# The order of modulation stores and loads, small loads in front of large ones, the routing's modulation on another engine, and a later ratio, in a fused transformer layer

## The chip, the cores and the metric

The kernel runs on one core of a Trainium2 chip. A core has a matrix engine (TensorE, PE in the profile), a vector engine (VectorE, DVE), an engine for activation functions (ScalarE, ACT), a general one (GpSimd, POOL) and one that issues transfers (SyncE, SP). Each works through its own instructions in order and waits on semaphores for the others. Transfers (DMA) run beside them; here SP and POOL issue nearly all. The metric is the device time of one execution in microseconds, lower is better.

## The reference, cut to what matters

Two layers on x of shape (4, 512, 288) float32 and a condition of shape (4, 288); 16 heads of 18 numbers, 4 experts, the best 2 per token.

```python
mod = silu(c) @ w_adaln + b_adaln
sh_msa, sc_msa, g_msa, sh_mlp, sc_mlp, g_mlp = split(mod, 6)
h = ln(x) * (1 + sc_msa) + sh_msa
q, k, v = h @ w_qkv + b_qkv
o = softmax(q k^T * 18**-0.5) v
x = x + g_msa * (o @ w_proj + b_proj)
xf = ln(x) * (1 + sc_mlp) + sh_mlp
logits = xf @ w_gate ; the two largest per token, softmax over them
moe = sum over the chosen experts of gate * (gelu(xf @ w1 + b1) @ w2 + b2)
x = x + g_mlp * moe
# second layer
U = qr(P).Q ; A = skew matrix filled with silu(cond) @ W.T + b ; R = expm(A)
x = x + (x U R - x U) U^T
```

## The kernel before, in words

The four sequences are called batches; each has four tiles of 128 tokens. x stays in SBUF as `xs`.

*Attention* is a loop over n = 4 b + g (batch b, group g of four heads), and in it over the four tiles t. A step (g, t) issues, in this order: `weigh` (PE's z products at L1779, ACT's exponentials es at L1788), `gather` of the step before (PE's av, L1797), the pieces of work that were put on the list `steps[g, t]`, one piece of the list `beside`, and one scatter (`scatter_next`), two where g is 0 or 3. This order of issue is each engine's order of execution. When the four tiles of a group are done, `normalize` takes the sums of the softmax out through SP (den), DVE takes reciprocals, SP stores them (rdr) and loads them spread over partitions (oT, L1833), and DVE multiplies (oT, L1839). When a batch has its four groups, `merge` (L1855 to L1865) multiplies with w_proj (po), DVE applies the gate (og) and POOL adds it to `xs`.

The work of batch b's steps contains the next batch's first layer norm and q, k, v (`beginning`), and the routing of the batch before (`routing`): `norm` at (2,1) with statistics on DVE (mv), four small instructions on POOL (rs, ms, L1169 to L1175), the normalized rows on ACT (xh, L1184) and the modulation on POOL (L1877 and L1880: times modrow, plus modrow, into xr); the logits in two halves at (2,2) and (2,3), each logit one product with a row of w_gate and its sum on DVE (L1921); the choice of experts at (3,0) (g, L1950, is the difference of the two best logits); `ratio` at (3,1), an exponential of it on ACT (L1954); the gates at (3,2). The second batch of a half (batches 0 and 1, batches 2 and 3) also computes `where`, the places of its tokens in a DRAM table `slots`, and then 16 scatters (L2110, indirect DMA on POOL) write the half's tokens there. Batch 2's routing thus runs in batch 3's steps, and batch 3's in the experts' phase.

The shifts, scales and gates of the modulation are computed twice: for the first norm ahead of the loop, and for the rest (`other_modulation`) as pieces of `beside` in batch 0: PE's pr and DVE's modrows (L1269), then `spread`, which takes four rows to DRAM (mdr, L1275) and back to all 128 partitions (modrow and gates, L1276), on POOL's queue. `skew_matrices`, also in `beside`, computes the skew matrices: `loads` issues the 2.27 MB of W (wr, L1295), a memset and two stores (um, udr), and four loads of the bias (brs, L1306), all on POOL's queue; `product` (pa) multiplies wr on PE. After it, in pieces of `beside` through the attention of batches 0 to 2, comes the matrix exponential (lines 1380 to 1500, tiles pw, XY, ph). A QR of P (`column`, L1558 to L1600) goes in pieces on DVE too.

POOL's DMAs use eight completion semaphores in turn, and an issue waits for the one eight before it, if that has not landed; SP's use eight others.

*Experts.* `hidden(i)` (ph, L2427) and `outputs(i)` (pe, L2487) for i = 0 to 7, four experts for each half of the tokens; tokens come from `slots` (xg, `load_slots`, L2166 to L2171, six DMAs; the first expert's on POOL's queue), are transposed on PE (pt, L2205), and results go back by scatter (chosen, L2503). `load_slots` of the first expert comes after all 16 scatters of the first half, at step (2,3) of batch 3. The list `last_merge` (last divisions, the merge of batch 3), then batch 3's routing, then the rest of the QR, are done one piece at a time in between. A last phase rotates the result and writes it (from about 700 us).

Of the kernel before, what the change touches and what calls it, by code (L numbers as in the profile page):

```python
# [13 lines left out]
ALU = mybir.AluOpType  # L14
# [4 lines left out]
P = 128  # L19
# [794 lines left out]
def fast_path(  # L814
# [142 lines left out]
    with ExitStack() as s1:  # L957
# [92 lines left out]
        def late_loads():  # L1050
            badr = ada.tile([P, C], F32, tag="raw", name="badr")
            nc.gpsimd.memset(badr, 0.0)
            badrs.append(badr)
            for i in range(4):
                nc.sync.dma_start(
                    out=badr[i * HQ : i * HQ + B, :],
                    in_=b_adaln[ds((2 + i) * C, C)].partition_broadcast(B),
                )
            for b in range(1, B):
                nc.sync.dma_start(  # L1060
                    out=xs[:, b * NT : (b + 1) * NT, :],
                    in_=x[b].rearrange("(t p) c -> p t c", p=P),
                )
            nc.sync.dma_start(out=bp, in_=b_proj.partition_broadcast(P))
            nc.sync.dma_start(out=wgT, in_=w_gate)
            nc.sync.dma_start(out=b1s, in_=b1T)
            nc.sync.dma_start(out=wp, in_=w_proj.rearrange("g p c -> p g c"))

        def shift_scale(between):
# [181 lines left out]
        def other_modulation():  # L1251

            rows = ada.tile([P, C], F32, name="modrows")
            mdr = dram.tile([4, B, C], F32, name="mdr")
            to = (gates[:, 0], modrow[:, 0], modrow[:, 1], gates[:, 1])

            def product():

                pr = bank([P, N], "pr")
                for k in range(NK):  # L1260
                    for i in range(4):
                        nc.tensor.matmul(
                            pr[ts(i, HQ), :C],
                            scp[:, k, :],
                            wadb[:, k, ts(i, C)],
                            start=(k == 0),
                            stop=(k == NK - 1),
                        )
                nc.vector.tensor_add(rows, pr[:, :C], badrs[0])  # L1269
                one = rows[2 * HQ : 3 * HQ, :]  # L1270
                nc.vector.tensor_scalar_add(one, one, 1.0)

            def spread():
                for i in range(4):
                    nc.gpsimd.dma_start(out=mdr[i], in_=rows[i * HQ : i * HQ + B, :])  # L1275
                    nc.gpsimd.dma_start(out=to[i], in_=mdr[i].partition_broadcast(P))  # L1276

            return [product, spread]

        def skew_matrices(between):  # L1280

            width = NV // 4
            right.close()
            skew = right.enter_context(tc.tile_pool(name="skew", bufs=1, side="right"))
            um = skew.tile([2 * D, BH, D], F32, name="um")
            udr = dram.tile([D, B, D], F32, name="udr")
            wr = skew.tile([CC, NK, NV], F32, name="wr")
            brs = skew.tile([P, width], F32, name="brs")  # L1290
            row = brs

            def loads():
                for i in range(4):
                    nc.gpsimd.dma_start(  # L1295
                        out=wr[:, :, ts(i, width)],
                        in_=wrT[:, ts(i, width)].rearrange("(k p) f -> p k f", p=CC),
                    )
                nc.gpsimd.memset(um, 0.0)
                for h in range(2):  # L1300
                    nc.gpsimd.dma_start(
                        out=udr[:, ts(h, BH), :], in_=um[ts(h, D), :, :]
                    )
                nc.gpsimd.memset(brs, 0.0)
                for i in range(4):
                    nc.gpsimd.dma_start(  # L1306
                        out=brs[i * HQ : i * HQ + B, :],
                        in_=br[ts(i, width)].partition_broadcast(B),
                    )

            def product():
                pa = bank([P, N], "pa")
                for k in range(NK):
                    for i in range(4):
                        nc.tensor.matmul(
                            pa[ts(i, HQ), :width],
                            scp[:, k, :],
                            wr[:, k, ts(i, width)],
                            start=(k == 0),
                            stop=(k == NK - 1),  # L1320
                        )
                nc.vector.tensor_add(row, pa[:, :width], brs)

            def stores(i, half):
                at, count = 0, 0
                for r in range(D - 1):
                    n = D - 1 - r
                    lo, hi = max(at, i * width), min(at + n, (i + 1) * width)
                    count += lo < hi
                    if lo < hi and count % 2 == half:  # L1330
                        nc.sync.dma_start(
                            out=udr[r, :, ds(r + 1 + lo - at, hi - lo)],
                            in_=row[i * HQ : i * HQ + B, ds(lo - i * width, hi - lo)],
                        )
                    at += n

            def load():
                for h in range(2):
                    nc.sync.dma_start(out=um[ts(h, D), :, :], in_=udr[:, ts(h, BH), :])

            def last():
                pt = bank([P, N], "ptA")
                for b in range(BH):
                    for h in range(2):
                        at = ts(h, D)
                        nc.tensor.matmul(
                            pt[at, ts(b, D)],
                            um[at, b, :],
                            ident[at, at],
                            start=True,  # L1350
                            stop=True,
                        )
                nc.vector.tensor_sub(
                    A.rearrange("p b d -> p (b d)"),
                    um.rearrange("p b d -> p (b d)"),
                    pt[:, : BH * D],
                )
                right.close()

            idle = [lambda: None]  # L1360
            return (
                [loads]
                + between
                + [product]
                + [lambda i=i: stores(i // 2, i % 2) for i in range(8)]
                + [load]
                + idle * 2
                + [last]
            )
# [499 lines left out]
        def route(b):  # L1869

            xr = rt.tile([P, NT, ROW], F32, tag="xr", name=f"xr{b}", bufs=B // HALVES)
            parts = statistics(b, 1)

            def norm():
                xh = normalized(b, 1, *parts)
                for t in range(NT):
                    nc.gpsimd.tensor_tensor(  # L1877
                        xh[:, t, :], xh[:, t, :], modrow[:, 1, b, :], ALU.mult
                    )
                    nc.gpsimd.tensor_tensor(  # L1880
                        xr[:, t, :C], xh[:, t, :], modrow[:, 0, b, :], ALU.add
                    )

            return [norm] + choose(b, xr)

        TH = BH * NT
        halves = {}
# [350 lines left out]
        vectors = gate_vectors()  # L2238
        beside = [lambda: None] + other_modulation() + [skew, prefetch]
        chain, basis = triangular()  # L2240
        held, divides = [], {}

        def gather_oldest():
            n, t, es = held.pop(0)
# [15 lines left out]
        def routing(b):  # L2260
            def start():
                norm, logits0, logits1, top, choices, ratio, gates_, *end = route(b)
                also((2, 1), norm)
                also((2, 2), logits0)
                also((2, 3), logits1)
                also((3, 0), top, choices)
                also((3, 1), ratio)
                also((3, 2), gates_, *end[:1])
                also((3, 3), *end[1:])

            return start
# [14 lines left out]
        for n in range(NN):  # L2286
# [47 lines left out]
                also((3, 2), *takes[:3])  # L2334
                also((3, 3), *takes[3:])
            for t in range(NT):
                if (n, t) == (NN - 2, NT - 1):

                    xg0 = load_slots(0, a2, "hT", 1, nc.gpsimd)
                held.append((n, t, weigh(n, t)))  # L2340
                if len(held) > 1:
                    gather_oldest()
                for piece in steps[g, t]:
                    piece()
                if beside:
                    beside.pop(0)()
                scatter_next()
                if g in (0, 3):
                    scatter_next()
        while held:  # L2350
            gather_oldest()
        for piece in beside:
# [5 lines left out]
            lambda: divide(NN - 1),  # L2358
            None,
            *merge(B - 1),  # L2360
        ]

        third.clear()
# [435 lines left out]
```

## Time and profile before

| | us |
|---|---|
| three runs | 729.96, 725.80, 729.78 (median 729.78) |
| profiled execution, its own time | 727.14 |
| span of its trace | 725.4 |
| busy: PE, DVE, ACT, POOL | 675.8, 487.0, 290.4, 251.4 |
| mean granted clock of PE | 0.969 |

The span is cut into stretches below: busy time of each engine, and the clock granted to PE (1.00 is full speed).

```profile
core 0: us, PE busy (x) PEld busy (x) DVE busy (x) ACT busy (x) POOL busy (x), PEclk, DMA share, GB/s
60.00:67.00 7.00, 1.74 (x16) 0.16 (x8) 1.50 (x7) 0.05 (x1) 3.44 (x7) 0.93 1.00 241
67.00:76.00 9.00, 3.85 (x16) 1.30 (x20) 4.10 (x21) 5.66 (x8) 4.91 (x10) 0.50 0.47 106
76.00:84.00 8.00, 8.00 (x68) 2.70 (x64) 6.19 (x30) 3.82 (x6) 7.01 (x14) 0.98 0.95 309
180.00:200.00 20.00, 17.68 (x94) 5.31 (x94) 17.88 (x92) 11.07 (x14) 4.48 (x9) 0.98 0.17 44
200.00:210.00 10.00, 10.00 (x48) 4.82 (x46) 7.67 (x33) 1.94 (x2) 0.89 (x2) 0.70 0.01 2
313.00:324.00 11.00, 1.57 (x6) 1.01 (x6) 9.93 (x49) 2.45 (x6) 7.19 (x9) 0.60 0.36 92
352.00:380.00 28.00, 28.00 (x125) 20.63 (x124) 14.93 (x63) 9.62 (x23) 10.47 (x14) 1.00 0.38 114
```

A row has the stretch, its length, busy time and number of instructions by engine, the granted clock, the share of time that the DMA engines moved data, and their rate. PE is nearly idle around 60 to 76 and 313 to 324 and full in the experts' phase (last row); the clock falls behind such gaps.

### The profile page before, as it was taken

The page shows a single profiled execution, that of the slowest core. Times are in us where ns is not written, and L with a number is a line of the kernel's source. Part 1 is how long each engine was busy: PE and PEld are TensorE (multiplying, and loading weights), DVE is VectorE, ACT ScalarE, POOL GpSimd, SP SyncE. Part 2 cuts the span into 40 slices and gives each one's busy share as a digit, 9 for nine tenths or more (in the row PEclk, how much of TensorE's full clock was granted, in tenths as well). Part 3 has the DMA queues.
Part 4 walks back from the last instruction along what each step waited for, and adds up shares of the span by engine and source line. Part 5 has one row for each costly group of instructions (what it writes and reads, how often), then busy time and mean ns, then how long its engine had stood idle before and what let it go on. Part 6 is the DMA issues. An engine that isn't in the chain of part 4 may idle for free. (4 is left out here: it accounts for less than half of the span.)

```text
span 725.4 us, 11487 instructions
## 1 busy us (share of the span) xinstructions
PE 675.8 (93%) x3563; PEld 391.0 (54%) x3563; DVE 487.0 (67%) x2172; ACT 290.4 (40%) x465; POOL 251.4 (35%) x382
## 2 busy tenths in 40 slices
PE   6994999989898999949999999999999999999985
PEld 5421332434242434215677776777667676667753
DVE  5473658586876995793179888988888885005144
ACT  3464556475528454734233323323232232222231
POOL 3025862461236337760155263522203132121110
PEclk9998899999989999969999999999999999999997
DMA  9457841001100113346152453355344053206053
GB/s 211 143 175 191 256 140 47 27 18 45 48 13 24 31 60 98 92 123 154 36 158 68 138 149 104 95 150 172 75 123 111 12 172 78 90 22 218 17 164 114
DMA packets 70530, 75.48 MB, mean 104 GB/s; under 512 B 33452, under 2 KB 57746, under 8 KB 70458
## 3 DMA queue, kind: packets, MB, share of 16 engines
q1 hardware_dynamic: 60166, 47.78, 24.1%
q0 software_dynamic: 9792, 26.45, 11.9%
q8 instruction: 30, 0.49, 0.3%
q10 hardware_dynamic: 500, 0.42, 0.3%
q14 instruction: 42, 0.34, 0.2%
HBM read 52.13 MB, written 18.23 MB: 97 GB/s over the span
## 5 line engine op out<-in xcount | busy, mean ns | idle before, releaser
L2487 PE MATMUL pe<-w2s,hm 128*128 128x288 f32 (+1 forms) x648 | 163.7, 408 | 0.0
L1788 ACT ACTIVATE es<-z 128x1024 f32<-128x1024 f32 x128 | 124.0, 1020 | 71.9 <-PE z L1779 71.7
L2427 PE MATMUL ph<-xgT,w1s 128*128 128x288 f32 (+2 forms) x576 | 151.8, 413 | 0.4
L2487 PEld LDWEIGHTS pe<-w2s,hm 128*128 128x128 f32 (+1 forms) x648 | 118.7, 187 | 31.5 <-issue 2.3
L2427 PEld LDWEIGHTS ph<-xgT,w1s 128*128 128x128 f32 x576 | 105.8, 190 | 40.0 <-issue 10.8
L1779 PE MATMUL z<-qk 32*128 32x512 f32 x512 | 92.9, 663 | 15.8 <-ACT es L1788 15.8
L2449 ACT ACTIVATE hm<-ph,b1r 128x576 f32<-128x576 f32 (+2 forms) x72 | 49.8, 737 | 130.4 <-PE ph L2440 125.0
L1797 PE MATMUL av<-es,vt 128*32 128x512 f32 x512 | 71.4, 631 | 0.0
L2502 POOL TENSOR_TENSOR y<-y,gb 128x288 f32<-128x288 f32 x32 | 26.1, 817 | 121.5 <-ACT y L2501 121.4
L1779 PEld LDWEIGHTS z<-qk 32*128 32x128 f32 x512 | 27.9, 189 | 60.0 <-ACT es L1788 44.9
L2501 ACT ACTIVATE y<-pe,weight 128x288 f32<-128x288 f32 x32 | 16.0, 501 | 104.0 <-PE pe L2487 104.0
L1741 PE MATMUL pq<-hT,wqk 96*126 96x512 f32 (+3 forms) x120 | 57.3, 615 | 0.0
L2503 POOL DMA_INDIRECT chosen<-y,place x36 | 36.6, 1016 | 53.9 <-DVE y L2499 34.3
L2110 POOL DMA_INDIRECT slots<-xr,where x32 | 32.5, 1016 | 60.4 <-DMA slots<-xr,where 35.6
L1921 DVE SCALAR_TENSOR_TENSOR pl<-xr,wg 128x288 f32<-128x288 f32 x64 | 46.0, 781 | 9.2 <-POOL xr L1880 9.2
L1561 DVE SCALAR_TENSOR_TENSOR q<-q 64x1 f32<-64x1 f32 (+1 forms) x192 | 46.2, 241 | 7.0
L1572 DVE STREAM_SHUFFLE wj<-pt 32x288 f32<-32x288 f32 (+47 forms) x96 | 42.1, 438 | 0.7
L1741 PEld LDWEIGHTS pq<-hT,wqk 96*126 96x126 f32 (+3 forms) x120 | 20.8, 184 | 34.2 <-issue 30.4
L1797 PEld LDWEIGHTS av<-es,vt 128*32 128x32 f32 x512 | 10.3, 110 | 50.4 <-issue 42.6
L1753 POOL DMA_DIRECT2D qk<-row x42 | 21.4, 516 | 45.1 <-ACT row L1748 45.0
L1855 PE MATMUL po<-wp,oT 128*128 128x288 f32 x128 | 34.7, 422 | 1.1 <-DVE oT L1839 1.1
L1839 DVE TENSOR_TENSOR oT<-oraw,oT 128x512 f32<-128x512 f32 x16 | 11.0, 689 | 36.5 <-DMA oT<-rdr 30.4
(281 smaller groups left out, 898.7 us busy)
## 6 DMA issues: line engine op xcount, KB each, us to landing
w2s<-in_w_dram SPq DMA_DIRECT2D x8, 1296.0 KB
w1s<-in_w_dram SPq DMA_DIRECT2D x8, 1152.0 KB
slots<-empty POOLq DMA_DIRECT2D x36, 148.0 KB, 3.5
oT<-rdr SPq DMA_DIRECT2D x64, 64.0 KB
qk<-row POOLq DMA_DIRECT2D x42, 72.0 KB, 2.6
yc<-chosen SPq DMA_DIRECT2D x4, 576.0 KB
out_dram<-xs SPq DMA_DIRECT2D x8, 288.0 KB
wr<-in_wrT_dram POOLq DMA_DIRECT2D x4, 567.0 KB, 8.9
```

Source lines behind the costliest of these rows:

```text
L1561: nc.vector.scalar_tensor_tensor(s, u, part, s, ALU.mult, ALU.add)
L1572: nc.vector.stream_shuffle(wj[o : o + HQ, j:], pt[o0 : o0 + HQ, j:], [j % HQ] * HQ)
L1741: nc.tensor.matmul(pq[:n], wqk[:rows, k, item, :n], hT[:rows, k, :], start=(k == 0), stop=(k == NK - 1),)
L1779: nc.tensor.matmul(zs[c // 2][:, c % 2, :], qk[ts(c, HQ), 1, ts(t, P)], qk[ts(c, HQ), 0, :], start=True, stop=True,)
L1788: nc.scalar.activation(e, z, AF.Exp, scale=SCALE)
L1797: nc.tensor.matmul(avs[n][ts(c, HQ), :], vts[b % 2][:, t, 4 * g + c, :], es[c // 2][:, c % 2, :], start=(t == 0), stop=(t == NT - 1),)
L1855: nc.tensor.matmul(po, oTs[b][:, g, ts(t, P)], wp[:, g, :], start=(g == 0), stop=(g == NG - 1),)
L1921: nc.vector.scalar_tensor_tensor(pr, xr[:, t, :C], 1.0, wg[:, e, :], ALU.mult, ALU.mult, accum_out=lg[:, t, e : e + 1],)
L2427: nc.tensor.matmul(ph[:, j, :SB], w1s[:, k, ts(f, P)], xgT[:, k, ts(j, SB)], start=(k == 0), stop=False,)
L2449: nc.scalar.activation(hm[:, f, : CAPS[r]].rearrange("p (j s) -> p j s", j=NB), ph[:, :, :SB], AF.Gelu_apprx_tanh, bias=b1r[:, h, r, f : f ...
L2487: nc.tensor.matmul(po[ts(m, rows), :], slots_[:, f, :], w[:, f, :], start=(f == 0), stop=(f == NF - 1),)
L2503: nc.gpsimd.indirect_dma_start(out=chosen[h], out_offset=bass.IndirectOffsetOnAxis(ap=place[:, t : t + 1], axis=0), in_=y, in_offset=None, ...
```

## The change

1. In `late_loads` (SP), w_gate, b_proj and b1 come in front of the loads of x for batches 1 to 3.
2. In `spread`, all four stores come first, then the four loads that read them back.
3. In `loads` of the skew matrices, the memset, the two small stores and the four bias loads come first, the four large loads of wr last.
4. In `route`, the modulation (two instructions for each of four tiles) is done by DVE, two tiles at a time in front of each half of the logits.
5. For batch 2 the ratio goes from (3,1) to (3,3), and the gates (`gates_`) to the end of `last_merge`; what follows in that list of pieces comes one piece later.
6. The first expert's `load_slots` goes from step (2,3) to (2,0) of batch 3, and two scatters are issued per step where g is 1, as well as 0 and 3, so that all 16 are issued before it.

```diff
@@ late_loads
+            nc.sync.dma_start(out=wgT, in_=w_gate)
+            nc.sync.dma_start(out=bp, in_=b_proj.partition_broadcast(P))
+            nc.sync.dma_start(out=b1s, in_=b1T)
             for b in range(1, B):
...
-            nc.sync.dma_start(out=bp, in_=b_proj.partition_broadcast(P))
-            nc.sync.dma_start(out=wgT, in_=w_gate)
-            nc.sync.dma_start(out=b1s, in_=b1T)
@@ spread
                 for i in range(4):
                     nc.gpsimd.dma_start(out=mdr[i], in_=rows[i * HQ : i * HQ + B, :])
+                for i in range(4):
                     nc.gpsimd.dma_start(out=to[i], in_=mdr[i].partition_broadcast(P))
@@ skew_matrices, loads
-                for i in range(4):
-                    nc.gpsimd.dma_start(
-                        out=wr[:, :, ts(i, width)],
-                        in_=wrT[:, ts(i, width)].rearrange("(k p) f -> p k f", p=CC),
-                    )
                 nc.gpsimd.memset(um, 0.0)
...
                         in_=br[ts(i, width)].partition_broadcast(B),
+                    )
+                for i in range(4):
+                    nc.gpsimd.dma_start(
+                        out=wr[:, :, ts(i, width)],
+                        in_=wrT[:, ts(i, width)].rearrange("(k p) f -> p k f", p=CC),
                     )
@@ route
             def norm():
-                xh = normalized(b, 1, *parts)
-                for t in range(NT):
-                    nc.gpsimd.tensor_tensor(
-                        xh[:, t, :], xh[:, t, :], modrow[:, 1, b, :], ALU.mult
-                    )
-                    nc.gpsimd.tensor_tensor(
-                        xr[:, t, :C], xh[:, t, :], modrow[:, 0, b, :], ALU.add
-                    )
-
-            return [norm] + choose(b, xr)
+                xhs_.append(normalized(b, 1, *parts))
+
+            def modulated(t):
+                xh = xhs_[0]
+                nc.vector.tensor_mul(xh[:, t, :], xh[:, t, :], modrow[:, 1, b, :])
+                nc.vector.tensor_add(xr[:, t, :C], xh[:, t, :], modrow[:, 0, b, :])
+
+            def with_logits(i, logits):
+                for t in range(i * NT // 2, (i + 1) * NT // 2):
+                    modulated(t)
+                logits()
+
+            chosen_ = choose(b, xr)
+            for i in range(2):
+                chosen_[i] = lambda i=i, logits=chosen_[i]: with_logits(i, logits)
+            return [norm] + chosen_
@@ routing
+                if b == B - 2:
+
+                    also((3, 0), top, choices)
+                    also((3, 3), ratio)
+                    late.append(gates_)
+                    return
@@ attention loop
-                if (n, t) == (NN - 2, NT - 1):
+                if (n, t) == (NN - 2, 0):
 
                     xg0 = load_slots(0, a2, "hT", 1, nc.gpsimd)
...
-                if g in (0, 3):
+                if g in (0, 1, 3):
                     scatter_next()
@@ last_merge
             *merge(B - 1),
+            *late,
         ]
```

More of the change, by code (lines that the diff above doesn't have):

```diff
@@ L1872, in route @@
             parts = statistics(b, 1)
+            xhs_ = []
             def norm():
-                xh = normalized(b, 1, *parts)
-                for t in range(NT):
-                    nc.gpsimd.tensor_tensor(
-                        xh[:, t, :], xh[:, t, :], modrow[:, 1, b, :], ALU.mult
-                    )
-                    nc.gpsimd.tensor_tensor(
-                        xr[:, t, :C], xh[:, t, :], modrow[:, 0, b, :], ALU.add
-                    )
-            return [norm] + choose(b, xr)
+                xhs_.append(normalized(b, 1, *parts))
[11 more added lines that the diff above has]
+            return [norm] + chosen_
         TH = BH * NT
@@ L2240, in fast_path @@
         chain, basis = triangular()
-        held, divides = [], {}
+        held, divides, late = [], {}, []
         def gather_oldest():
```

## Prediction, made before the changed kernel had run

> **What bounds the kernel now.** I read the busy times first, then the waits of TensorE, then each stretch of the timeline where TensorE is idle or its granted clock falls.
>
> ```profile
> PE 675.8 (93%) x3563; PEld 391.0 (54%) x3563; DVE 487.0 (67%) x2172; ACT 290.4 (40%) x465; POOL 251.4 (35%) x382
> PEclk9998899999989999969999999999999999999997
> ```
>
> TensorE (PE) has work for 93% of the span, so the change can pay only in the 50 us without PE work, or where the clock row falls below 9. The waits say which these are.
>
> ```profile
> PE z L1779 <- ACT es L1788: 15.8, 13, 10.4
> PE pt L2205 <- DVE q L1558: 7.0, 1, 7.0
> PE pt L2205 <- DMA xg<-slots: 2.7, 1, 2.7
> PE ph L1436 <- DVE XY L1474: 2.1, 1, 2.1
> PE pt L1205 <- DVE pw L1452: 1.3, 1, 1.3
> PE pt L1205 <- DVE XY L1488: 0.9, 1, 0.9
> ```
>
> So one wait of 10.4 us on ACT, three small ones on DVE (4.3 us together), and 9.7 us in front of the experts (L2205). The timeline by engine at the first and the last place:
>
> ```profile
> 56.47 2.75 POOL L1295 DMA_DIRECT2D wr<-in_wrT_dram  x4 [0.35 <-PE av L1797]
> 63.91 0.52 POOL L1306 DMA_DIRECT2D brs<-in_br_dram  x1 [1.21 <-DMA wr<-in_wrT_dram]
> 69.00 2.18 ACT L1184 ACTIVATE xh<-xs,ms,rs 128x288 f32<-128x288 f32 x4 [8.96 <-POOL ms L1175]
> 72.14 2.98 PE L1779 MATMUL z<-qk 32*128 32x512 f32 x8 [10.41 <-ACT es L1788]
> ...
> 297.70 0.24 POOL L1175 TENSOR_SCALAR ms<-ms 128x4 f32<-128x4 f32 x1
> 316.54 0.21 ACT L1954 ACTIVATE g<-g 128x4 f32<-128x4 f32 x1 [5.99 <-DVE g L1950]
> 314.73 0.93 POOL L2166 DMA_DIRECT2D xg<-slots  x1 [3.98 <-DMA slots<-xr,where]
> ```
>
> (Start, duration, engine, instruction; in brackets the idle time before it and who ended it.) At 60 us POOL is held by the small brs loads, which wait for wr's landings, so its four statistics instructions (rs, ms) are late, ACT's xh is late, and with ACT in order the softmax behind it. From 60 to 72 PE does 1.7 us of work, and the granted clock is 0.50 from 66.5 to 76.2. At 313 ACT waits 5.99 us for the routing's g; the experts' first tokens (xg) wait behind the scatters.
>
> **Start of attention.** The interleaved store-load pairs (39.2 to 55.6) go in a row: four stores at 0.6 us to 41.6, then four loads at 0.6 us. The first store landed 2.0 us after its issue ended, so the loads run 42.1 to 44.6 instead of ending at 56.1. um, udr and two brs loads follow to about 48; two more brs and the wr loads each reuse a completion flag of a load eight earlier, which landed 4.2 and 3.9 us after issue before. wr's first issue is thus 49.3 and its last ends by 53.5 (in before 56.47 to 63.9). rs starts there, ms comes 2 us later: 55.5, and with wr issued as late as 57 still 59.7. ACT is free for xh at 60.05, so its wait goes. z follows xh by 3.14 us in before (69.00 to 72.14): z at 63.2, 9.0 us earlier, and the 1.3 us that half clock cost up to 79 go too: **-10.2**.
>
> What is late next: wr itself. Its 2.27 MB took 14 us from first issue to quiet engines (56.5 to 70.5). From 49.3 that is 63.3, from 53.5 it is 67.5; the skew product that reads it came 4.4 us behind z's restart, now 67 or so. Nearer to the early end, as the first two issues alone keep the engines busy: nothing lost, at worst 4 us. Moving small loads in front of x's loads at 30 us: three issues of 0.4 to 0.7 us, 1.6 us; batch 1's statistics ended at 53.3 and are not used before 53.5: nothing.
>
> [...]
>
> **Routing of batches 0 and 1.** Eight modulation instructions per batch go from POOL to DVE, each pair in front of its logits.
>
> ```profile
> 150.03 1.03 DVE L1921 SCALAR_TENSOR_TENSOR pl<-xr,wg 128x288 f32<-128x288 f32 x1 [2.05 <-POOL xr L1880]
> 161.09 0.45 DVE L1921 SCALAR_TENSOR_TENSOR pl<-xr,wg 128x288 f32<-128x288 f32 x1
> 158.14 0.64 PE L1205 MATMUL pt<-ident,xh 128*96 128x128 f32 x4 [1.27 <-DVE pw L1452]
> 199.75 0.69 PE L1436 MATMUL ph<-XY,pw 64*64 64x64 f32 x8 [2.15 <-DVE XY L1474]
> ```
>
> The same logit takes 1.03 us while POOL runs its TENSOR_TENSORs and 0.45 (0.385 from start to start) once POOL has stopped. So 16 x 0.385 = 6.2 plus 8 x 0.40 = 3.2 (from DVE's 0.69 us for 512 columns; 0.46 for 288 in L1864) is 9.4 us, against 15.0 (148.0 to 163.0) now: DVE is 5 us ahead from there. The waits of 1.27 and 2.15 us go: DVE runs without a gap from 179 to 205, starting behind the oT of 179.15, whose chain moves by 4.4 us. With the second goes the clock of 0.50 that the windows show from 199.6 to 206; at half clock the eight av matmuls took 1.94 instead of 1.06, so about 2.5 of the 6.4 us. For batch 1 the wait of 0.94 us at 236 goes: **-1.3 -2.15 -2.5 -0.9 = -6.9**. Bounds: if the two waits are set by other chains, only -2; not below -9.
>
> [...] The idle 2.15 us was enough for the 6.4 us at 0.50. [...]
>
> **End of attention.** Three things move. The ratio of batch 2 goes two steps later and its gates behind the last merge: ACT's 5.99 us wait goes, three small DVE pieces (1.4 us) enter phase 2, under PE work. Modulation leaves POOL (7.3 us). And the first expert's loads, six issues, 7.3 us, go from step (2,3) to (2,0) of the last group pair, behind all 16 scatters of the first half; for that two scatters go per step in g = 1 as well. In POOL's order the last three scatters and two residual additions now stand in front of the rs and ms of batch 2.
>
> ```profile
> 294.87 1.01 POOL L2110 DMA_INDIRECT slots<-xr,where  x1 [1.17 <-DMA slots<-xr,where]
> 298.90 2.17 ACT L1184 ACTIVATE xh<-xs,ms,rs 128x288 f32<-128x288 f32 x4
> 347.11 0.69 DVE L1839 TENSOR_TENSOR oT<-oraw,oT 128x512 f32<-128x512 f32 x1 [5.17 <-DMA oT<-rdr]
> ```
>
> Each scatter waits for the one before: 1.0 issued and 1.8 landing, 2.8 us. Three more make 8.4, less 2 us of holes already there: ms at 304.3 instead of 297.94, and xh, without wait at 298.90 now, waits **5.4 us**, PE's softmax step behind it; some 6 us of PE idle. In return, of the 10.4 us in front of the experts all but a little goes: the experts start near 324.7 instead of 330.55, 5.9 earlier. But the merge of batch 3, 16 us into them, needs the last oT (347.11), which hangs on a chain of divisions and small DMAs (recip at 325.4, stores, loads, recip at 336, stores, loads) behind the last attention steps. PE reaches that product (346.47) just in time now, so it would come 3 to 5 us too early, and only 0.6 to 2.6 us of the 5.9 stay, with a half-clock stretch to pay (up to 2.5 us, as above). I take **0** (-3 to +3).
>
> From there to the end PE is full (20 of 20 us per window), POOL and DVE have slack there, and the last 25 us are the same chain: everything before shifts through.
>
> **Sum.** -10.2 - 6.9 + 0 = -17.1 on the profiled execution's 727.14 us (span 725.4): 710.0. That execution lies 2.6 us under the median of the runs shown (729.78) and 1.3 over the lowest; I put the forecast at 711.
>
> **Rivals.**
> *End of attention repaired too.* If scatters shrink behind the earlier `where`, and ms is not later, the 10.4 us and their half clock (0.50 to 328.6) go: -12.9 more, 698. Against it: the 2.8 us cadence in every pair of scatters; for it: where moves 0.7 to 1.7 us ahead of PE.
> *wr's landing becomes the wait.* If the loads to modrow and gates land late, now four together, wr's flags come late; at 57 as the first issue wr is there at 71, and the skew product costs 4 us and a half clock of 1 to 3. Then -4 to -6 from the first stage: 715 to 717; with routing's lower bound, 720.
> *DVE becomes the bound* (slower). If the 1.03 us is not POOL's doing but these operands', modulation costs as much: 24 x 0.97 = 23 us per routing instead of 15. Then PE waits 8 us more at 158, at 236 and at the end, with 2.5 of half clock each, +31 against -10: 748. It decides from 19 us per routing (0.79 per instruction), where three times 4 us more eat the first stage. Against it: 0.45 as soon as POOL stops.
> *The change does nothing where it counts*: POOL stays held by another flag, statistics as late as now: 725 to 732.
>
> **From these to the numbers.** Chances: forecast 0.52; full repair 0.15; wr late 0.20; DVE bound 0.06; nothing 0.07. The forecast's own range is 705 to 716. Downwards the range takes half of the repair (700), upwards all of wr late with routing's lower bound and some spread between runs (723); out remain half of the repair, DVE and nothing: 0.2. One per cent, 7.3 us, is about what a measurement of this kernel tells from no change. Faster by more: 0.52 + 0.15 + most of wr late (0.15), 0.82; within: 0.11; slower: 0.07.
>
> **What would show it.** Right: no wait of ACT's xh near 60, z of step (2,2) near 63, clock near 1 from 60 to 80; logits at 0.4 us in every routing, no wait at XY; a new wait of about 5 us of ACT on ms near 285, the 7.0 and 2.7 us waits gone, and one of 3 to 5 us at po in front of the last oT. Wrong: skew's product waiting for wr, logits still at 1 us, or scatters closer than 2.8 us.

## The result, and the profile after

The changed kernel took 724.03 us (median of 20 runs, 720.63 to 728.21), the kernel before 727.75 us (20 runs, 722.37 to 729.96): a ratio of 0.9957, with a 95% interval of 0.9939 to 0.9976. That is 3 us faster, real but small; 711 us (700 to 723) were predicted. The profiled execution of the changed kernel has a span of 723.0 us, against 725.4.

The waits of TensorE in the changed kernel (what waited, for whom; us in total, times, longest):

```profile
PE z L1780 <- ACT es L1789: 14.1, 14, 8.2
PE po L1856 <- DVE oT L1840: 9.2, 3, 6.6
PE pt L1205 <- DVE brs L1323: 5.6, 1, 5.6
```

All the waits that the change was predicted to remove are gone: the 10.4 us on es, the 2.1, 1.3 and 0.9 us on VectorE, the 9.7 us in front of the experts. Three others stand in their place: 8.2 us on es at another spot, 6.6 us on the last oT, and 5.6 us on the addition of the skew product (brs). The first was foreseen at 6 us, the second at 3 to 5 us, the third not at all.

Where the gain went can be followed by the start of the same TensorE instruction in the two traces:

| TensorE instruction | before | after | difference |
|---|---|---|---|
| first z (no part of the change has acted yet) | 28.05 | 26.72 | -1.3 |
| z, first after the long wait | 72.14 | 61.75 | -10.4 |
| skew product pa | 76.55 | 65.42 | -11.1 |
| z two steps on | 82.27 | 72.12 | -10.2 |
| z after the transposes | 89.99 | 86.74 | -3.2 |
| z in batch 1 | 163.28 | 159.86 | -3.4 |
| z in batch 2 | 209.19 | 202.29 | -6.9 |
| z in batch 3, ahead of the norm of batch 2 | 298.18 | 290.17 | -8.0 |
| the next z, behind it | 302.03 | 301.41 | -0.6 |
| first product of the experts | 330.55 | 318.89 | -11.7 |
| po, second tile of the last merge | 350.66 | 347.81 | -2.9 |
| end of the span | 725.4 | 723.0 | -2.4 |

The 1.3 us at the top are there before anything differs between the kernels and belong to the execution, so each later difference has that much less of the change in it. Nine us were won at 62 us, seven of them lost by 87; five were won in the routings; seven lost at 300; eleven won back in front of the experts, nine of them lost at po. Less the 1.3 us, these two traces end 1.1 us apart, the medians 3.7: a single pair of executions is no better than that.

The first loss, in the timelines of GpSimd, SyncE, VectorE and TensorE of the changed kernel (start, duration, engine, instruction, idle time before it and who ended it):

```profile
50.99 0.73 POOL L1307 DMA_DIRECT2D wr<-in_wrT_dram  x1 [0.96 <-DMA modrow<-mdr]
53.86 2.02 POOL L1307 DMA_DIRECT2D wr<-in_wrT_dram  x3 [2.14 <-DMA gates<-mdr]
57.77 0.25 POOL L1175 TENSOR_SCALAR ms<-ms 128x4 f32<-128x4 f32 x1
...
56.07 0.35 SPq L1826 DMA_DIRECT2D rdr<-den  x1
65.84 1.72 SPq L1834 DMA_DIRECT2D oT<-rdr  x4
...
72.38 0.69 DVE L1840 TENSOR_TENSOR oT<-oraw,oT 128x512 f32<-128x512 f32 x1 [10.34 <-DMA oT<-rdr]
79.39 0.68 DVE L1323 TENSOR_TENSOR brs<-pa,brs 128x504 f32<-128x504 f32 x1 [0.18 <-DMA slots<-empty]
...
61.75 2.04 PE L1780 MATMUL z<-qk 32*128 32x512 f32 x8 [1.35 <-ACT es L1789]
65.42 3.69 PE L1316 MATMUL pa<-wr,scp 96*32 96x504 f32 x24
80.13 1.09 PE L1205 MATMUL pt<-ident,xh 128*96 128x128 f32 x4 [5.65 <-DVE brs L1323]
```

W is issued at 51 to 56 us, ms is ready at 58, z starts at 61.75 and pa does not wait: as predicted. But the 8 KB store rdr of the first division, issued at 56.07, has landed only when the oT loads can be issued at 65.84, and these only at 72.38. VectorE stands 10.34 us in front of that division, and behind it in its order are a QR column, the next group's reciprocal and the addition that empties pa's bank. TensorE's transposes need that bank at 74.5 and get it at 80.1.

The second loss, in the timelines of GpSimd, ScalarE and TensorE, and the third, in those of SyncE, VectorE and TensorE, of the changed kernel:

```profile
294.90 0.98 POOL L2119 DMA_INDIRECT slots<-xr,where  x1 [1.78 <-DMA slots<-xr,where]
297.69 0.54 POOL L1175 TENSOR_SCALAR ms<-ms 128x4 f32<-128x4 f32 x1
298.27 2.18 ACT L1184 ACTIVATE xh<-xs,ms,rs 128x288 f32<-128x288 f32 x4 [7.26 <-POOL ms L1175]
301.41 2.98 PE L1780 MATMUL z<-qk 32*128 32x512 f32 x8 [8.22 <-ACT es L1789]
...
329.51 0.57 SPq L1826 DMA_DIRECT2D rdr<-den  x1
330.17 0.38 SPq L2175 DMA_DIRECT2D xg<-slots  x1
330.60 7.60 SPq L2177 DMA_DIRECT2D xg<-slots  x4
338.88 1.86 SPq L1834 DMA_DIRECT2D oT<-rdr  x4
342.40 0.69 DVE L1840 TENSOR_TENSOR oT<-oraw,oT 128x512 f32<-128x512 f32 x1 [7.26 <-DMA oT<-rdr]
343.15 1.33 PE L1856 MATMUL po<-wp,oT 128*128 128x288 f32 x2 [6.62 <-DVE oT L1840]
```

ms stands behind the sixteenth scatter. And the four loads of the last oT stand on SP's queue behind six loads of the second expert's tokens, which take 8.6 us to issue.

### The profile page after: what moved, and what is told of

The parts are those of the page before. It is cut to its first block, busy times and chain, and to the rows that moved or that the text cites. A ratio compares the mean times of both kernels' runs of the same rounds, so it can differ in the third digit from the quotient of the medians.

```text
span 723.0 us, 11477 instructions
## 1 busy us (share of the span) xinstructions
PE 674.6 (93%) x3563; PEld 391.4 (54%) x3563; DVE 485.3 (67%) x2204; ACT 290.2 (40%) x465; POOL 223.3 (31%) x350
## 5 line engine op out<-in xcount | busy, mean ns | idle before, releaser
L1780 PE MATMUL z<-qk 32*128 32x512 f32 x512 | 90.7, 650 | 14.1 <-ACT es L1789 14.1
L1562 DVE SCALAR_TENSOR_TENSOR q<-q 64x1 f32<-64x1 f32 (+1 forms) x192 | 44.3, 231 | 7.0
L1798 PEld LDWEIGHTS av<-es,vt 128*32 128x32 f32 x512 | 10.2, 109 | 48.8 <-issue 40.3
L1856 PEld LDWEIGHTS po<-wp,oT 128*128 128x128 f32 x128 | 23.5, 191 | 22.4 <-DVE oT L1840 10.6
```

The costliest lines, as they stand in the source:

```text
L1562: nc.vector.scalar_tensor_tensor(s, u, part, s, ALU.mult, ALU.add)
L1780: nc.tensor.matmul(zs[c // 2][:, c % 2, :], qk[ts(c, HQ), 1, ts(t, P)], qk[ts(c, HQ), 0, :], start=True, stop=True,)
L1798: nc.tensor.matmul(avs[n][ts(c, HQ), :], vts[b % 2][:, t, 4 * g + c, :], es[c // 2][:, c % 2, :], start=(t == 0), stop=(t == NT - 1),)
L1856: nc.tensor.matmul(po, oTs[b][:, g, ts(t, P)], wp[:, g, :], start=(g == 0), stop=(g == NG - 1),)
```

## Experiments

Times below are medians; ratios are to runs of the kernel before on the same chip (725.0 to 727.9 us), with 95% intervals. The changed kernel has 0.9957 (0.9939 to 0.9976). Four runs (the divisions behind the addition, a third of W, the last oT first, four together) ran where the kernel before had 725.0 us, 2.7 less than beside the changed kernel; for these the differences to the changed kernel are taken from the ratios.

**Only the transfers' order.** The kernel before with the first three hunks of the change's diff (`late_loads`, `spread`, `loads`), of which the core is

```diff
                 for i in range(4):
                     nc.gpsimd.dma_start(out=mdr[i], in_=rows[i * HQ : i * HQ + B, :])
+                for i in range(4):
                     nc.gpsimd.dma_start(out=to[i], in_=mdr[i].partition_broadcast(P))
```

> The kernel before with only the transfers' order changed (parts 1 to 3). Theory: TensorE's attention steps come 10 us earlier from 62 us on, but only some 3.2 us are left from 90 us on, as in the changed kernel (z at 128.1 for 131.3 before): VectorE stands at its first division until the small loads behind W have landed (72 us), and the addition that frees the skew product's bank comes behind that. Time: 3 us under the kernel before. Rival, as predicted: the 10 us go through to the end, 10 us under it.

723.3 us, 0.9944 (0.9913 to 0.9975), 4 us under the kernel before. The wait at the addition is there:

The waits of TensorE in this kernel:

```profile
PE pt L2206 <- DVE q L1559: 6.8, 1, 6.8
PE pt L1205 <- DVE brs L1323: 6.8, 1, 6.8
```

Of the 10 us only 3 to 4 stay, as the theory had it; going through to the end would have been 717. The 6.8 us in front of the experts are still there too.

**Only the modulation on VectorE.** The kernel before with the hunk of `route`:

```diff
-                    nc.gpsimd.tensor_tensor(
-                        xh[:, t, :], xh[:, t, :], modrow[:, 1, b, :], ALU.mult
-                    )
...
+                nc.vector.tensor_mul(xh[:, t, :], xh[:, t, :], modrow[:, 1, b, :])
```

> The kernel before with only the routing's modulation on VectorE (part 4). Theory: logits at 0.45 us, no wait of TensorE at pw or XY, 4.5 to 5 us won by 240 us; and with GpSimd free of it at 302 to 310, the last scatters end and the first expert's loads issue some 7 us earlier with no new wait of ms, another 3 to 6 us. Time: 8 to 11 us under the kernel before, more than the whole change. Rival, that the end of attention is bound by something else and gives all back: 4 to 5 us under it or the same.

716.3 us, 0.985 (0.979 to 0.991): 11 us under the kernel before and 8 under the changed kernel. This one part is worth more than the whole change. The windows of this kernel behind 200 us (length; busy time by engine; granted clock; DMA share; GB/s):

```profile
200.00:210.00 10.00, 8.21 (x43) 4.60 (x40) 7.99 (x31) 3.27 (x4) 2.21 (x4) 1.00 0.02 2
```

The clock is 1.00 here, 0.70 before: the half clock behind XY's wait is gone. At the end of attention, without part 6, GpSimd's last scatter is issued at 299.9 us (309.7 before) and the first expert's loads at 303.3 (314.7), with no new wait on ms.

**Part 6 taken back.**

```diff
-                if (n, t) == (NN - 2, 0):
+                if (n, t) == (NN - 2, NT - 1):
...
-                if g in (0, 1, 3):
+                if g in (0, 3):
```

> The changed kernel with part 6 taken back (scatters at the old pace, the first expert's loads at step (2,3)). Theory: three scatters fewer stand in front of rs and ms, so ScalarE's wait of 7.3 us and TensorE's of 8.2 us near 293 us go; a wait for xg of up to 5 us comes in front of the experts, and the last division comes 5 to 8 us earlier. Time: 4 to 9 us under the changed kernel. Rival, that the early loads are worth what the scatters cost: the same as the changed kernel or slower.

717.0 us, 0.986 (0.979 to 0.993), 7 us under the changed kernel. GpSimd's and ScalarE's timelines in this kernel:

```profile
291.61 0.24 POOL L1175 TENSOR_SCALAR ms<-ms 128x4 f32<-128x4 f32 x1
292.32 1.10 POOL L2119 DMA_INDIRECT slots<-xr,where  x1 [0.47 <-issue]
...
292.15 2.18 ACT L1184 ACTIVATE xh<-xs,ms,rs 128x288 f32<-128x288 f32 x4
```

ms comes 6 us earlier, ScalarE does not wait, and TensorE waits 7.0 us (4.3 and 2.7) in front of the first expert's tokens instead. The place of the scatters is the cause of the second loss.

**The QR column behind the addition.**

```diff
-                    for step in ((1, 0), (1, 3), (2, 1), (2, 3)):
+                    for step in ((1, 0), (1, 3), (2, 3)):
                         also(step, column)
...
+                if b == 0:
+                    also((3, 3), column)
```

> The changed kernel with one QR column of batch 0 (5.7 us on VectorE), which stands between the late division and the addition of the skew product, moved from step (2,1) to (3,3). Theory: the addition follows the division of 72.4 us within 2 us instead of 7, TensorE's wait of 5.65 us at the transposes and the half clock behind it go, 6 to 7 us earlier from 90 us on. Time: 5 to 7 us under the changed kernel. Rival, that these transposes wait for W or for the clock and not for VectorE's order: the same as the changed kernel.

722.2 us, 0.9921 (0.9895 to 0.9947): 2 us under the changed kernel, where 5 to 7 were expected, and the intervals overlap. The wait fell from 5.65 to 2.71 us, not to nothing: behind the division (72.2) the reciprocal waited until 74.8 for the next group's sums, whose loads are queued on SP behind the late oT loads. So it is VectorE's order that TensorE waits for, and it is not the column alone.

**The divisions behind the addition.**

```diff
+                    if (b, i) == (0, 2):
+                        for m in (0, 1):
+                            also((2, 3), lambda m=m: divide(m))
+                        continue
+                    if (b, i) == (0, 3):
+                        also((3, 0), lambda: divide(1))
+                        also((3, 1), lambda: divide(1))
...
```

> The changed kernel with the first two groups' divisions put behind the addition of the skew product in VectorE's order (steps (2,3) to (3,1) of batch 0). Theory: the addition follows the product (69.1 us), TensorE's wait at the transposes (5.65 us, 2.7 with only the column moved) goes wholly with its half clock, and z of batch 1's first steps comes 6 to 7 us earlier than in the changed kernel; 3 to 6 us under it in the end, since the end of attention keeps part. Rival, that the transposes wait for something else too: as with the column moved, 2 to 3 us.

Two of its four executions took 723.4 and 724.2 us, the other two 949.5 and 2044.0 us, for which nothing in its profile gives a reason; the kernel before had 725.0 us there, and only the profile is used. The addition ran at 69.07, the wait at the transposes was gone and z came at 79.58 instead of 86.74, as expected. But none of it reached the end. TensorE's timeline in batch 1:

```profile
124.30 4.71 PE L1856 MATMUL po<-wp,oT 128*128 128x288 f32 x10 [6.00 <-DVE oT L1840]
```

The first batch's merge waits for its last division. That chain (VectorE's reciprocals, SyncE's small transfers) was hardly made earlier (124.30 for 125.47 in the changed kernel); only TensorE was let past it. The edit itself also puts two divisions later, so this run alone does not show where the chain would end without it. What it does show is that letting one consumer past the queue uncovers the next.

**A third of W.** This leaves out two thirds of W's loads; the product multiplies one third three times, so the rotations differ.

```diff
-                        out=wr[:, :, ts(i, width)],
-                        in_=wrT[:, ts(i, width)].rearrange("(k p) f -> p k f", p=CC),
+                        out=wr[:, 0, ts(i, width)],
+                        in_=wrT[:CC, ts(i, width)],
```

> The changed kernel with a third of W loaded (0.76 MB for 2.27; the skew product multiplies that third three times, so the rotations differ). Theory: the small stores and loads of the divisions (rdr, oT) then land soon after their issue near 56 us, VectorE's first division comes before 66 us instead of at 72.4, the addition of the skew product right behind it, and TensorE's wait of 5.65 us with its half clock is gone: 6 to 7 us earlier from 90 us on; 4 to 7 us under the changed kernel in the end. Rival, that W's bytes do not hold the small ones: the division near 72 us as now, and the same time.

716.6 us, 0.9884 (0.9807 to 0.9962): by the ratios 5 us under the changed kernel, though the two intervals just overlap. SyncE's and VectorE's timelines in this kernel:

```profile
55.34 0.35 SPq L1826 DMA_DIRECT2D rdr<-den  x1
57.58 1.72 SPq L1834 DMA_DIRECT2D oT<-rdr  x4
...
64.07 0.69 DVE L1840 TENSOR_TENSOR oT<-oraw,oT 128x512 f32<-128x512 f32 x1 [2.98 <-DMA oT<-rdr]
71.00 0.68 DVE L1323 TENSOR_TENSOR brs<-pa,brs 128x504 f32<-128x504 f32 x1 [0.19 <-DMA slots<-empty]
```

rdr to oT takes 2.2 us instead of 9.8, VectorE divides at 64.07 instead of 72.38, TensorE does not wait at the transposes, and the gain stays: the first merge product comes 10.0 us earlier than before (3.2 in the changed kernel). With the same order and fewer bytes the loss is gone, so it is W's burst that holds the small transfers.

**W early and alone.** The four broadcast loads of the modulation go behind rs, ms and the gate weights; W follows the four modulation stores and the two stores of udr, ahead of the loads of the bias.

```diff
+            def back():
                 for i in range(4):
                     nc.gpsimd.dma_start(out=to[i], in_=mdr[i].partition_broadcast(P))
...
+                for i in range(4):
+                    nc.gpsimd.dma_start(
+                        out=wr[:, :, ts(i, width)],
...
+        vectors[1] = lambda turn=vectors[1]: (turn(), back())
```

> The changed kernel with the whole W, issued right behind the four modulation stores (near 42 us instead of 51 to 56), and the four broadcast loads of the modulation (2.3 MB) behind rs and ms and the gate weights (near 60 us). Theory: W has landed before the first division's store is issued (56 us), so rdr and oT land in their usual 2 to 5 us, VectorE divides before 66 us, and TensorE's wait of 5.65 us is gone as with a third of W: z of the step at 86.7 comes at 80; 5 to 8 us under the changed kernel, near 717. Rival, that any 2 MB beside the division do the same (now the broadcast loads): the division near 70 us again and the time of the changed kernel.

722.1 us, 0.9931 (0.9893 to 0.9968), 2 us under the changed kernel with overlapping intervals, where 5 to 8 were expected. W went out at 45.4 to 48.1, and rdr to oT took 1.4 us (59.42 to 60.86), as the theory says. But W now covered the loads of the sums (VectorE waited 6.99 us for den, until 59.14), and the broadcast loads at 61 to 63 us covered oT (69.30). The division came near 70 us again, as the rival has it: in this run the small transfers beside either large load were late. Between 45 and 70 us there are 5.1 MB of large ones (four of 567 KB, five of 576). TensorE's wait at the transposes fell to 2.6 us.

**The last oT first on SP's queue.**

```diff
-                if m == 1 and i + 1 < HALVES * E:
+                if i and m == 1 and i + 1 < HALVES * E:
                     xg = load_slots(i + 1, hp, "xg", 1)
                 if rest and (piece := rest.pop(0)):
                     piece()
+                if not i and m == 1:
+                    xg = load_slots(i + 1, hp, "xg", 1)
```

> The changed kernel with the four loads of the last oT issued on SP's queue in front of the second expert's six loads instead of behind them. Theory: the last division comes some 7 us earlier (335 for 342.4), TensorE's wait of 6.6 us at po and the half clock behind it go; 5 to 9 us under the changed kernel. Rival, that the last oT hangs on the division's sums and not on SP's order: the same as the changed kernel.

720.1 us, 0.9928 (0.9892 to 0.9965): by the ratios 2 us under the changed kernel with overlapping intervals, so the time alone shows no gain (one execution of ten took 1302 us, unexplained). The wait at po fell from 6.62 to 3.78 us. It is the queue, as the theory says, but less of it than the 7 us expected. What is left is the store in front of oT: rdr is issued at 331.05, half a us behind the 1.3 MB load of the second matrix (w2s), whose traffic ends near 336.2, and oT can be issued only at 337.52. It looks like the start of attention again, a small transfer beside a large one; the best kernel below moves that load too.

**Four of these together.** The divisions behind the addition, part 6 taken back, the last oT first, and the first expert's weights one step later.

```diff
-                weights = [expert_weights(0)]
+                weights = []
+                also((3, 1), lambda: weights.append(expert_weights(0)))
```

> The changed kernel with the divisions behind the addition, part 6 taken back, the last oT's loads in front of the second expert's, and the first expert's weights issued one step later (they start with the last scatter, whose landing they delay). Theory: the gains of these places add: -6 at the start, -7 from the scatters, -3 from the last oT, 3 or so from the first tokens: 708, 14 to 19 us under the changed kernel. Rival, that each only uncovers the next wait: 715 to 718, as part 6 taken back alone.

716.2 us, 0.9879 (0.9801 to 0.9956), by the ratios 6 us under the changed kernel: the rival. TensorE reached the first expert's tokens at 306.9 and waited 7.48 us for them. The weights moved later did not help: they were now issued at 306.6, among the tokens' own loads (301.4 to 308.6), and the transposes of the tokens could go on at 314.8, with part 6 alone taken back at 313.6.

**W early, and the end of attention rearranged.** Part 6 taken back; the first expert's tokens on SP's queue; the second matrix and the second expert's tokens behind the last oT.

```diff
-                    xg0 = load_slots(0, a2, "hT", 1, nc.gpsimd)
+                    xg0 = load_slots(0, a2, "hT", 1)
...
-        weights2 = [expert_weights2(0)]
+        weights2 = []
...
+                if not i and m == 1:
+                    weights2.append(expert_weights2(0))
+                    xg = load_slots(i + 1, hp, "xg", 1)
```

> The run with W early, and at the end of attention part 6 taken back, the first expert's tokens issued on SP's queue (six issues of 0.4 us there, 0.9 on GpSimd's), and the second matrix and the second expert's tokens behind the last oT. Theory: no wait of ScalarE on ms, TensorE's wait for xg 2 to 4 us instead of 7, none at po; 702 to 708, 16 to 22 us under the changed kernel. Rival, that the waits only change their place: 710 to 717.

710.0 us, 0.9749 (0.971 to 0.9789): 14 us under the changed kernel and 18 under the kernel before, the best of all, but short of the 702 to 708 expected and at the edge of the rival's range. The waits on ms and for xg are gone; those at po are not: 1.6 us are left at the last oT, and 4.3 us at the first batch's merge. SyncE's and TensorE's timelines:

```profile
299.49 0.39 SPq L2177 DMA_DIRECT2D xg<-slots  x1
299.93 3.46 SPq L2179 DMA_DIRECT2D xg<-slots  x4
...
306.92 0.63 PE L2216 MATMUL pt<-ident,xg 128*128 128x128 f32 x4 [0.34 <-DMA xg<-slots]
```

With the last, at 303.43, six issues take 4.5 us on SP's queue instead of 7.3 on GpSimd's, and the tokens cost TensorE 0.34 us.

**Part 5 taken back, twice.** Parts 1 to 4 only (parts 5 and 6 taken back), and the best kernel without part 5:

```diff
-                if b == B - 2:
...
-                    also((3, 3), ratio)
-                    late.append(gates_)
-                    return
```

> The changed kernel with parts 5 and 6 taken back (the kernel before with parts 1 to 4). Theory: parts 5 and 6 are what costs, and of them part 6: 716 to 718, as with part 6 alone taken back (717.0). Rival, that part 5 is worth something by itself: 720 or more; or that parts 1 to 3 and part 4 add (4 and 11 us): 712 to 713.

> The run with W early and the end of attention rearranged (710.0), with part 5 taken back as well, so that of the change parts 1, 2, 3 and 4 are left. Parts 1 to 4 alone had 714.6 and part 6 alone taken back 717.0, their intervals overlapping. Theory: part 5 is worth nothing where ScalarE does not wait for it: 709 to 711. Rival: it costs the 2 to 3 us between those two: 706 to 708.

Parts 1 to 4 took 714.6 us, 0.9818 (0.9769 to 0.9868), 9 us under the changed kernel; so parts 5 and 6 together cost 9 us, and part 6 alone 7 (717.0). Whether part 5 cost the rest cannot be told from those intervals. In the best kernel neither expectation held: without part 5 it took 715.0 us, 0.9826 (0.9784 to 0.9868), 5 us more. ScalarE's and TensorE's timelines without part 5:

```profile
311.20 0.20 ACT L1965 ACTIVATE g<-g 128x4 f32<-128x4 f32 x1 [8.50 <-DVE g L1961]
...
312.37 2.99 PE L1782 MATMUL z<-qk 32*128 32x512 f32 x8 [5.53 <-ACT es L1791]
```

Where the tokens were late, the ratio's wait showed no cost, since TensorE waited in front of them anyway (4.6 and 2.7 us with parts 1 to 4 only); with the tokens there at 306, ScalarE's wait for g at (3,1) is what TensorE waits for, 5.5 us. Part 5 is worth 5 us there, with the other wait gone.

## Why the prediction was wrong, point by point

*Start of attention, predicted -10.2, measured -1.9 (the -3.2 of the table less the 1.3 of the execution).* The mechanism was right to within a microsecond as far as it went: stores at 0.6 us, the waits on modrow's and gates' flags (1.05, 0.96 and 2.14 us), ms at 57.8 (predicted 55.5, at most 59.7), z at 61.75 (63.2), pa at 65.4 with no wait for W. The step that failed is "what is late next: wr itself", answered with "nothing lost, at worst 4 us". It asked only when W lands for its own product. That small loads amid W took 10 us could be seen in the trace before (oT's four loads of 64 KB were issued from 59.98 to 61.90, and VectorE could divide at 71.50); the question who waits for them, and who is queued behind that waiter on VectorE, was not asked. VectorE's timeline in the kernel before had the answer:

```profile
71.50 0.69 DVE L1839 TENSOR_TENSOR oT<-oraw,oT 128x512 f32<-128x512 f32 x1 [9.83 <-DMA oT<-rdr]
79.39 0.68 DVE L1322 TENSOR_TENSOR brs<-pa,brs 128x504 f32<-128x504 f32 x1 [1.15 <-DMA slots<-empty]
```

VectorE stood at the same division until 71.50 (72.38 in the changed kernel), behind the same W, and came to the addition at 78.2. There it waited 1.15 us more; the view names a DMA, but the skew product had ended just then, at 79.26. The change brought the product eleven us forward and left VectorE where it was: the addition starts at 79.39 in both traces. So TensorE could gain only as far as the transposes that need the addition's bank (84.57 before, 80.13 after, -4.4, of which 1.3 are the execution's), and another 1.2 went with the half clock behind the new wait (0.50 from 80 to 84). Moving W did not put it beside the division; it was there already, and the change left it there. The run with a third of W shows it: there the division comes 8 us earlier and 6.8 us come back at the first merge.

In the changed kernel rdr was issued at 56.07, behind all of W (51 to 55.9), W's traffic ends at 64.5 us, and oT is issued at 65.84. In the kernel before the same store went out at 55.86, ahead of W's first load (56.47), and oT could be issued at 59.98; late there were oT's own loads, issued amid W. Whether rdr's own bytes were late or only the signal that they had landed, no run here separates.

*Routings, predicted -6.9, measured -4.8 (from -3.2 to -8.0).* Right in mechanism: the logit takes 0.45 us and the modulation 0.45, all waits of TensorE on pw and XY are gone and the clock is 1.00 where it was 0.70. Sizes: of the 1.3 us, a wait of 0.63 us for hT took half; behind the 2.15 us there came 1.39 us at po. Some of the size is chance: each trace has one stretch of half clock here that the other has not (at 146 us after, at 227 us before; see the last section), and the two about cancel. The rival "VectorE becomes the bound" is out: the slow logits are GpSimd's doing, not that of their operands, and the changed kernel shows it once more. VectorE's timeline in batch 3's steps, and GpSimd's:

```profile
306.58 1.04 DVE L1930 SCALAR_TENSOR_TENSOR pl<-xr,wg 128x288 f32<-128x288 f32 x1
310.48 0.45 DVE L1930 SCALAR_TENSOR_TENSOR pl<-xr,wg 128x288 f32<-128x288 f32 x1
...
306.42 3.82 POOL L1850 TENSOR_TENSOR xs<-xs,gb 128x288 f32<-128x288 f32 x4
```

For just as long as GpSimd's four additions last, the logits take 1.04 us again.

*End of attention, predicted 0 (-3 to +3), measured +5.2 (from -8.0 to -2.9).* All three mechanisms were named: the stall of ms (5.4 predicted, 7.26 measured; on TensorE 6 and 8.2), the experts earlier (5.9 and 3.7 in their own frame, -8.0 to -11.7), the wait at po (3 to 5 and 6.6). The term that was mis-sized is the last oT. It was to keep 0.6 to 2.6 us of gain; it lost 3.3 (347.11 to 342.40 is -4.7, against -8.0 for what lies in front). SyncE's timeline of that place in the kernel before:

```profile
336.30 0.34 SPq L1825 DMA_DIRECT2D rdr<-den  x1
337.36 5.12 SPq L2168 DMA_DIRECT2D xg<-slots  x4
343.15 2.03 SPq L1833 DMA_DIRECT2D oT<-rdr  x4
```

The late xh pushes VectorE's logits and its next reciprocal (324.84 to 321.33, only -3.5), but most of that is made up by the last store of the chain (rdr, 336.30 to 329.51, -6.8). The larger loss is behind it: on SP's queue the six token loads in front of oT took 8.6 us from the first to the end instead of 6.3, so oT's loads start at 338.88 for 343.15, -4.3. The prediction took that chain to stay where it was.

*Rivals.* "wr's landing becomes the wait" was close to what happened, but at the wrong consumer: pa did not wait at all, the small transfers did. Its upper end, 720, is 4 us under the time; the range ends 1 us under it, and the forecast lies 13 under it.

## What to carry to other kernels

When a large transfer is moved, list the small ones beside it, where it was and where it will be, the engine that waits for each, and what is queued behind that wait; here its own consumer never waited. Before counting a gain on one engine, look up in the trace before when the other engines reach what it will need next: the addition at 79.39 stood there. Work that comes earlier on a queue can hold up what stands behind it there: in the changed kernel ScalarE waited 7.26 us for ms behind three scatters more, and VectorE 7.26 us (5.17 before) for the last oT behind six loads; a part that won 11 us alone ended in a change of 3. Two waits on the same spot can hide each other: part 5 showed no gain while the tokens were late (714.6 us without it, 717.0 with it), and was worth 5 us when they came early.

## What the runs showed of the hardware

Behind a wait of 1.35 us TensorE's clock fell to 0.50 in one of these traces and stayed at 1.00 in the other. A wait of that length in front of z lies at the same place in both kernels (146.87 before, 143.68 after). In the windows, the first line of the kernel before, the others of the changed kernel:

```profile
148.00:149.00 1.00, 1.00 (x9) 0.24 (x10) 0.00 (x0) 1.00 (x3) 0.67 (x1) 1.00 0.09 8
```

```profile
146.00:147.00 1.00, 1.00 (x8) 0.00 (x0) 0.93 (x5) 1.00 (x3) 0.00 (x0) 0.50 0.00 0
148.00:149.00 1.00, 1.00 (x8) 0.86 (x10) 1.00 (x6) 0.42 (x1) 0.00 (x0) 0.50 0.19 61
149.00:150.00 1.00, 1.00 (x12) 0.16 (x8) 1.00 (x7) 0.15 (x1) 0.00 (x0) 0.96 0.43 133
```

Behind it the clock stayed at 1.00 in the kernel before; in the changed kernel it was 0.50 for 3.4 us (0.84 in the window from 145 to 146, 0.50 in three, 0.96 in the next: 0.3 + 3 + 0.1). Elsewhere it was the other way round: behind a wait of 1.25 us in front of z (224.78 before, 217.88 after) the next eight av matmuls took 1.93 us in the kernel before and 1.07 in the changed one. So here the price of a wait of 1 to 2 us could not be told beforehand to better than 1 to 2 us. What decides it, no run here showed.
